# A one-core block of WKV, 1-bit FFN, cross attention and ternary layer: the last attention's first 256 tokens ahead, two norms rearranged, half of the boot's weight sums on VectorE

## The chip, the cores and the metric

The kernel runs on one core of one Trainium2 chip. Its engines are TensorE (PE in the profile, with its weight loads as PEld), VectorE (DVE), ScalarE (ACT), GpSimd (POOL) and SyncE (SP), which issues the DMAs. The metric is the device time of one execution in microseconds (us), lower is better. Before the change the median of three runs is 1129.53 us (1128.88 to 1131.5).

## The reference

Four residual layers over `x` of (4, 512, 512), that is batch, tokens, channels, with a context of the same shape. Cut to what is computed:

```python
x = x + tanh(g_xattn[0]) * wkv(w, u, layernorm(x), ctx)        # scan over the tokens, each channel by itself
x = x + tanh(g_ffn[0])   * ffn_1bit(layernorm(x), w1, w2, w3)
x = x + tanh(g_xattn[1]) * attention_int8(layernorm(x), ctx)
x = x + tanh(g_ffn[1])   * ternary(x, gamma, W)

# ffn_1bit: bitlinear(x, w) = quant(x) @ (sign(w) * mean|w|).T
#           quant: groups of 64 channels, int8 by the group's max
#           h = silu(bitlinear(x, w1)) * bitlinear(x, w2); bitlinear(h, w3)
# attention_int8: q = qdq(x) @ qdq(wq).T + bq; k, v = split(ctx @ wkv.T + bkv)
#           16 heads of 32; softmax(q k^T / sqrt(32)) v; qdq(o) @ qdq(wp).T + bp
# ternary:  rms = rsqrt(mean(x*x) + 1e-6); xn = x * rms * gamma
#           a_scale = 127 / (max|xn| + 1e-5); round(xn * a_scale) / a_scale
#           @ (W rounded to -1, 0, 1 by mean|W|).T
```

The hidden width of the FFN is 2048; w1, w2 and w3 are fp32, 4 MB each.

## The kernel before

**Tiles and stages.** A batch's 512 tokens are four tiles `t` of 128 tokens by 512 channels, held in `xb`. The four batches go through WKV, FFN, attention and the ternary layer; neighbouring layers of neighbouring batches overlap. The first part, the boot, also makes the weights: `Weights.fetch` loads pieces `(m, f)` of 1 MB of w1, w2, w3 (m = 0, 1, 2; f = 0 to 3) into the tile `wn` (two buffers), `signs` writes the signs, `magnitudes` sums |w| with four ACT Abs passes with accumulation (L331), `turned` transposes the signs (`wt_ps`, L316 on ACT or L318 on DVE) and stores them to `wD`. `up_scales` needs the sums of all pieces of w1 and w2: `mean` adds them on DVE (L370), TensorE adds over the partitions (`tot_ps`), and L365 and L376 make the scales that the FFN's first activation needs. `Context.load(b)` transposes the context (`ct_ps`, L455); `keys_values(b)` makes keys (`k_ps`, split by ACT L272 and DVE L273, stored to `kD`) and values (`v_ps`, L534, stored to `vD`), and the attention loads them from there.

**WKV.** `wkv_layer` takes chunks of 128 channels: exponentials on ACT, scans on DVE (L625), the quotient (L631, L636), then TensorE transposes the chunk's result back (`wy_ps`) and DVE adds it to `xb` (L644). After chunk 3 come the layer norm's statistics and `rsqrt`, and with its scale and shift `ln_r` (L219, L220) ACT makes `ff_xn` (L224). The FFN quantises it (L231 group maxima, L671 to int8, ACT L675 back to bf16, POOL L676 times the scale), transposes it (`tp_ps`) and multiplies (`ff_hp`).

**Norm helpers.** `layernorm` makes statistics (L207, L210), a variance (L213, L214) and `rsqrt`: a shift and a subtraction as the first guess, then three Newton steps, all small DVE operations (L185 to L195). `centred` applies scale and shift on ACT (L224), `centred_aside` on POOL (L228). `absmax` is a DVE reduction (L231). `rounded` (ACT L246) multiplies by a scale and adds a magic number, `transposed_rows` transposes on TensorE (`qr_ps`) and takes the number off again (ACT L253).

**Attention.** `prepared` normalises a tile on POOL, takes absmax, rounds and transposes it; `project(g)` makes two head pairs of queries and stores them to `qD`. A unit `(p, h)` is a pair of heads p (0 to 7) over one half h of the tokens: 16 units per batch, in the order (0,0), (0,1), (1,0) and so on. The loop runs k = 0 to 17 and does in turn `scores(k)` (`s_ps`, DVE max L938, ACT exp L940), `values(k-2)` (`o_ps`, ACT copy L980), `turned(k-1)` (`pt_ps`, copied by ACT L960 and, in the last batch, by DVE L958 for one head of each pair) and `collect(k-2)` (`ot_ps`, DVE reciprocal L996 and product L998 into `at_o`). Each k has four yields. Keys of a pair are loaded by `fetch_keys` (tile `at_kR`, two buffers) when the pair before them has its h = 0; queries two units ahead; values for two pairs at a time. `project_out(t)` quantises `at_o` and multiplies by the output weights (`p_ps`), makes `at_y` (L1031) and adds it to `xb` (L1032), on POOL for batches 0 to 2, on DVE for the last.

**Ternary layer.** `ternary(t)` makes `tf_xn`: centred with scale and shift (POOL L228, in the last batch ACT L224), times gamma (L1110, POOL or, in the last batch, DVE), then absmax into `tf_s` (L231), small steps (L1115 to L1118), `rounded`, `transposed_rows`, `f_ps`, and L1128 with the store. For batches 0 to 2 this runs beside the next batch's layers; for the last batch `end((0, 1))` and `end((2, 3))` do `project_out`, layer norm and ternary for two tiles each, staggered by one step, after the unit loop. So after the last collect both halves of the tokens are still to be done.

**What sets the order.** A hand-made planner runs generators. Each has due places: `at_us` and `at_unit` for the boot, and slots (1/17 of a batch) afterwards; `run` always takes the generator whose next step is due first. TensorE's instructions are chained in that order in groups (`next_turn`). The other engines' order is made by a scheduler, but instructions given to `tc.keep_in_program_order` stay where the program has them. Each engine executes its own list in order, so an instruction that waits holds those behind it.

Of the kernel before, what the change touches and what calls it, by code (L numbers as in the profile page):

```python
# [10 lines left out]
F32 = mybir.dt.float32  # L11
# [19 lines left out]
def kernel(  # L31
# [150 lines left out]
    def rsqrt(v, n):  # L182
# [13 lines left out]
            y = y2  # L196
        return y

    def layernorm(xb, rms=False, tiles=range(NT), pinned=False):
# [20 lines left out]
        nc.vector.scalar_tensor_tensor(r[:, 1, :], mv[:, :, 0], -1.0, y, ALU.mult, ALU.mult)  # L220
        return {t: (r[:, 0, i : i + 1], r[:, 1, i : i + 1]) for i, t in enumerate(tiles)}
# [5 lines left out]

        nc.gpsimd.tensor_scalar(dst, xb[:, t, :], r[t][0], r[t][1], ALU.mult, ALU.add)  # L228

    def absmax(dst, src):  # L230
        nc.vector.tensor_reduce(dst, src, AX.X, ALU.max, apply_absolute_value=True)  # L231

    def quantise(dst, src, rscale, lo, hi=127.0):

# [56 lines left out]
    class Weights:  # L291
# [35 lines left out]
        def magnitudes(self, m, f, after=None):  # L327

            wn = self.raw.pop((m, f))
            for j in range(NC):  # L330
                ins = nc.scalar.activation(  # L331
                    wn[:, j, :],
                    wn[:, j, :],
                    AF.Abs,
                    accum_out=self.asum[:, m, f, j : j + 1],
                )
                if after is not None:
                    behind(ins, after)
# [492 lines left out]
    def attention_layer(b, xb, pool, tiles=range(NT)):  # L831
# [18 lines left out]
        def prepared(t, r):  # L850
            xn = row("at_xn")
            centred_aside(xn, xb, r, t)
            s = sm.tile([P, 2], F32, name="at_s", tag="at_s")
            yield True
            absmax(s[:, 0:1], xn)
            int8_scale(s[:, 0:1], s[:, 1:2], s[:, 0:1])
            rounded(xn, s[:, 1:2])
            yield True
            transposed_rows(xqT[:, :, t * P : (t + 1) * P], xn)
            sp = bank("sx_ps")[:, 0:P]  # L860
            transpose(sp, s[:, 0:1].to_broadcast([P, P]), ident)
# [47 lines left out]
            return slice(64 * (p % 2), 64 * (p % 2) + 64)  # L909

        def fetch_keys(p):
            kR[p] = pool.tile([P, 2, T], F32R, name="at_kR", tag="at_kR")
            stack(kR[p], kD[b][p // 2][:, pair(p), :], (0, 1, 0, 1))

# [8 lines left out]
            nc.sync.dma_start(out=V[g], in_=vD[b][:, :, g * P : (g + 1) * P])  # L923

        units = [(p, h) for p in range(NP) for h in range(len(tiles) // 2)]

        def scores(k, i, t):

# [86 lines left out]
        def project_out(t):  # L1015
            s = sm.tile([P, 2], F32, name="at_s", tag="at_s")
            o = o_all[:, t, :]
            absmax(s[:, 0:1], o)
            int8_scale(s[:, 0:1], s[:, 1:2], s[:, 0:1])
            rounded(o, s[:, 1:2])  # L1020
            yield True
            oqT = pool.tile([P, NC, P], BF16, name="at_oqT", tag="at_oqT")
            transposed_rows(oqT, o)
            yield True
            pp = bank("p_ps")
            for c in range(NC):
# [3 lines left out]
            y = row("at_y")  # L1030
            nc.vector.scalar_tensor_tensor(y, pp, s[:, 0:1], swp_b, ALU.mult, ALU.mult)  # L1031
            (nc.vector if alone else nc.gpsimd).tensor_tensor(  # L1032
                xb[:, t, :], xb[:, t, :], y, ALU.add
            )
            yield True
# [9 lines left out]
        def end(ts):  # L1045

            yield from together([project_out(t) for t in ts])
            r = layernorm(xb, rms=True, tiles=ts)
            yield from together([ternary(b, xb, pool, t, r) for t in ts])


        ahead, behind_it = end((0, 1)), end((2, 3))
        ending = in_steps([ahead, behind_it], 1)

        for k in range(len(units) + 2):
            now, before = k < len(units), 0 < k <= len(units)
# [10 lines left out]
            if alone and k > len(units):  # L1069
                next_turn()  # L1070
                next(ahead)
            yield
            for i in range(2):
                if now:
                    scores(k, i, 1)
            yield
            for i in range(2):
                if before:
                    turned(k - 1, i, 1)
            next_turn()  # L1080
            if k > 1:
                collect(k - 2)
            if now:
                p, h = units[k]
                if h == 0:
                    if p + 1 < NP:
                        fetch_keys(p + 1)
                    if p % 2 == 0 and p // 2 + 2 < NC:
                        next_turn()
                        project(p // 2 + 2)  # L1090
                elif p % 2 and p // 2 + 1 < NC:
                    fetch_values(p // 2 + 1)
                if k + 2 < len(units):
                    fetch_queries(k + 2)
            yield
# [7 lines left out]
    def ternary(b, xb, pool, t, r):  # L1103

        last = b == NB - 1
        if r is None:
            r = layernorm(xb, rms=True, tiles=[t])
        xn = pool.tile([P, D], F32, name="tf_xn", tag="at_row", bufs=ROWS)
        (centred if last else centred_aside)(xn, xb, r, t)
        (nc.vector if last else nc.gpsimd).tensor_tensor(xn, xn, gamma_b, ALU.mult)  # L1110
        s = sm.tile([P, 3], F32, name="tf_s", tag="tf_s")
        if not last:
            yield True
        absmax(s[:, 0:1], xn)
        nc.vector.tensor_scalar(s[:, 0:1], s[:, 0:1], 1e-5, None, ALU.add)  # L1115
        nc.vector.reciprocal(s[:, 1:2], s[:, 0:1])
        nc.vector.tensor_scalar(s[:, 1:2], s[:, 1:2], 127.0, None, ALU.mult)
# [3 lines left out]
        xT = pool.tile([P, NC, P], BF16, name="tf_xT", tag="at_oqT")  # L1121
        transposed_rows(xT, xn)
        yield True
        fp = bank("f_ps")
# [5 lines left out]
        yield True  # L1130

    def ternary_layer(b, xb, pool):
        r = layernorm(xb, rms=True)
        yield from in_steps([ternary(b, xb, pool, t, r) for t in range(NT)], 1)

# [42 lines left out]
    with (  # L1178
# [19 lines left out]
        def at_unit(n):  # L1198
# [98 lines left out]
    for b in range(NB):  # L1297
        if b:
# [12 lines left out]
            (b + 1 + 1.7 / SLOTS, b + 1 + 3.7 / SLOTS, 4),  # L1311
            (b + 1 + 3.75 / SLOTS, b + 1 + 4.35 / SLOTS, 2),
            (start, end, 72),
            (end, end + 2.4 / SLOTS, 6),
            (end + 2.4 / SLOTS, end + 3.4 / SLOTS, 4),
        )
        if b < NB - 1:
            line(
                late(lambda b=b: ternary_layer(b, xs[b], at)),
                (end + (3 if b < NB - 2 else 4.5) / SLOTS, end + (8 if b < NB - 2 else 12) / SLOTS, 7),  # L1320
                aside=True,
            )
    run(NB + 9)

# [44 lines left out]
```

## Time and profile before

| what | value |
|---|---|
| median of three runs | 1129.53 us (1128.88 to 1131.5) |
| the profiled execution, its own time | 1129.12 us |
| its span in the trace | 1127.3 us |
| mean granted TensorE clock | 0.954 |
| PE / PEld busy | 962.9 / 678.1 us |
| DVE / ACT / POOL busy | 877.7 / 721.4 / 308.8 us |
| first FFN matmul of batch 0 (`ff_hp` on the chain) | 102.31 us |
| last collect of batch 3 (`at_o` L998) starts | 1091.27 us |

The span is cut into 40 slices of 28.2 us in the page's second part, and each digit there is a busy share in tenths. "Idle before" an instruction is the time its engine stood, with what ended it. In the chain of waits each line is a start, a length, and the engine and line that held the end up. Busy shares over the whole span average over stages with different limits, so the stages are read by windows.

The last attention's 16 units end, by the start of the collecting DVE product, at 1004.00, 1010.08, 1015.24, 1020.74, 1026.16, 1032.44, 1042.96, 1049.16, 1055.68, 1061.88, 1068.02, 1073.34, 1079.10, 1084.54, 1088.85 and 1091.27 us.

### The profile page before, as it was taken

How to read it: one execution, taken by the hardware profiler on the slowest of the kernel's cores; microseconds unless marked ns; L12 is line 12 of the kernel's file. 1: busy time of each engine (PE TensorE's matmuls, PEld its weight loads, DVE VectorE, ACT ScalarE, POOL GpSimd, SP SyncE). 2: the span in 40 equal slices, each digit the busy share in tenths (PEclk: the TensorE clock that was granted, in tenths of full speed). 3: DMA queues.
4: the chain of work that ended last, by engine and by line, in shares of the span. 5: the costliest groups of instructions: out<-in, count | busy, mean ns of one | idle time of the engine just before them, and what ended most of it. 6: DMA issues, size and time to landing. Idle time of an engine off the chain costs nothing.

```text
span 1127.3 us, 16575 instructions
## 1 busy us (share of the span) xinstructions
PE 962.9 (85%) x5548; PEld 678.1 (60%) x5548; DVE 877.7 (78%) x1885; ACT 721.4 (64%) x1482; POOL 308.8 (27%) x301
## 2 busy tenths in 40 slices
PE   3878898988878978899998797999999899888983
PEld 2344565555546656676776475777777677555651
DVE  5857547769877799998769899978689766688776
ACT  5677655453224677667767676777676677877763
POOL 3821004333104143531215536212122400112000
PEclk9888999998888999999999999999999999998996
DMA  8188854443434654645555554464674572333401
GB/s 279 38 291 302 295 193 150 177 177 149 149 120 151 225 189 155 217 159 175 191 187 182 164 182 169 152 208 150 218 214 146 187 233 60 113 104 104 130 2 38
DMA packets 85668, 189.58 MB, mean 168 GB/s; under 512 B 12240, under 2 KB 36816, under 8 KB 74576
## 3 DMA queue, kind: packets, MB, share of 16 engines
q1 hardware_dynamic: 85584, 188.53, 49.7%
q8 instruction: 44, 0.72, 0.3%
q14 instruction: 40, 0.33, 0.1%
HBM read 148.65 MB, written 39.85 MB: 167 GB/s over the span
## 4 chain that ended last, share of the span: by engine, by line
PE 43%; DVE 29%; ACT 13%; issue 5%; POOL 4%; DMA 4%; SPq 1%; ACTq 0%; POOLq 0%; DVEq 0%
PE ff_hp L168 13%; PE ff_acc L168 6%; PE pt_ps L171 5%; PE o_ps L168 4%; DVE at_nm L938 3%; PE v_ps L168 3%; DVE wk_q L631 3%; PE s_ps L168 3%; ACT at_P L940 3%; DVE qg_i L671 2%; PE tp_ps L171 2%; ACT at_PT L960 2%; PE qr_ps L171 2%; ACT wk_e L603 1%; DMA wn<-in_L_ffn_w_dram 1%
## 5 line engine op out<-in xcount | busy, mean ns | idle before, releaser
L168 PE MATMUL ff_hp<-wT,xp 128*128 128x512 f32 x1024 | 272.3, 410 | 3.1 <-ACT at_P L940 2.1
L168 PEld LDWEIGHTS ff_hp<-wT,xp 128*128 128x128 f32 x1024 | 195.4, 195 | 51.9 <-ACT at_P L940 4.4
L940 ACT ACTIVATE at_P<-s_ps,at_nm 128x512 f32<-128x512 f32 x256 | 174.8, 690 | 64.8 <-DVE at_nm L938 63.4
L938 DVE TENSOR_REDUCE at_nm<-s_ps 128x1 f32<-128x512 f32 x256 | 165.8, 677 | 27.1 <-PE s_ps L168 26.7
L676 POOL TENSOR_TENSOR ff_z<-qg_b,qg_s 128x512 f32<-128x512 bf16 x64 | 71.2, 1112 | 378.9 <-ACT qg_b L675 326.3
L171 PE MATMUL pt_ps<-ident,at_P 128*128 128x128 f32 x1024 | 142.0, 279 | 12.5 <-ACT at_os L980 5.1
L960 ACT COPY at_PT<-pt_ps 128x512 f32<-128x512 f32 x224 | 125.0, 596 | 39.1 <-PE pt_ps L171 38.4
L171 PEld LDWEIGHTS pt_ps<-ident,at_P 128*128 128x128 f32 x1024 | 113.9, 141 | 54.7 <-issue 13.9
L168 PE MATMUL ff_acc<-wT,hr 128*128 128x512 f32 x512 | 136.7, 408 | 6.3 <-DVE hr L688 3.3
L168 PE MATMUL s_ps<-at_kR,at_qR 128*128 128x512 f32 x256 | 97.2, 448 | 19.9 <-ACT at_P L940 12.7
L168 PEld LDWEIGHTS ff_acc<-wT,hr 128*128 128x128 f32 x512 | 92.4, 190 | 27.4 <-DVE hr L688 4.6
L736 ACT ACTIVATE ff_z<-ff_hp,coef 128x512 f32<-128x512 f32 x64 | 43.9, 686 | 68.7 <-PE ff_hp L168 65.6
L168 PE MATMUL o_ps<-at_PT,at_V 128*32 128x256 f32 x1024 | 72.6, 397 | 1.6 <-ACT at_PT L960 0.9
L675 ACT CAST qg_b<-qg_i 128x512 bf16<-128x512 int8 x80 | 49.4, 617 | 34.2 <-DVE qg_i L671 24.7
L741 DVE SCALAR_TENSOR_TENSOR ff_z<-ff_hp,coef,ff_z 128x512 f32<-128x512 f32 x64 | 47.6, 744 | 28.3 <-PE ff_hp L168 28.1
L168 PE MATMUL v_ps<-wkvT,cT 128*128 128x512 f32 x128 | 63.4, 643 | 5.0 <-DVE wT L318 1.8
L168 PEld LDWEIGHTS s_ps<-at_kR,at_qR 128*128 128x128 f32 x256 | 45.6, 194 | 35.9 <-ACT at_P L940 20.7
L168 PE MATMUL k_ps<-cT,wkvT 128*128 128x512 f32 x128 | 62.3, 637 | 3.1 <-ACT cT L455 1.4
L737 DVE SCALAR_TENSOR_TENSOR ff_z<-ff_z,ff_hp 128x512 f32<-128x512 f32 x64 | 43.5, 679 | 25.7 <-ACT ff_z L736 25.7
L687 ACT CAST hr<-tp_ps 128x512 fp32r<-128x512 f32 x64 | 37.6, 588 | 33.9 <-PE tp_ps L171 33.9
L631 DVE RECIPROCAL wk_q<-wk_q 128x256 f32<-128x256 f32 x32 | 54.3, 1718 | 1.4 <-POOL wk_p L619 1.4
L171 PE MATMUL tp_ps<-ident,ff_z 128*128 128x128 f32 x256 | 40.3, 281 | 14.9 <-ACT at_PT L960 5.8
(177 smaller groups left out, 1749.7 us busy)
## 6 DMA issues: line engine op xcount, KB each, us to landing
wT<-wD SPq DMA_DIRECT2D x72, 1024.0 KB, 5.3
wn<-in_L_ffn_w_dram SPq DMA_DIRECT2D x18, 1024.0 KB, 7.3
at_kR<-kD SPq DMA_DIRECT2D x128, 128.0 KB, 3.5
at_qR<-qD SPq DMA_DIRECT2D x256, 64.0 KB, 2.2
wD<-wT SPq DMA_DIRECT2D x12, 1024.0 KB, 4.5
kD<-k_half SPq DMA_DIRECT2D x16, 512.0 KB, 3.3
qD<-at_half SPq DMA_DIRECT2D x32, 256.0 KB, 2.1
cn<-in_ctx_dram SPq DMA_DIRECT2D x8, 512.0 KB, 5.9
```

The lines of the kernel that those rows point to most:

```text
L168: return in_turn(nc.tensor.matmul(*args, **kwargs))
L171: return in_turn(nc.tensor.transpose(*args))
L631: nc.vector.reciprocal(half, half)
L675: nc.scalar.copy(qb, qi)
L676: nc.gpsimd.tensor_tensor(grouped(src), grouped(qb), s.unsqueeze(2).to_broadcast([P, NG, GS]), ALU.mult)
L687: nc.scalar.copy(part[:, 0, :], pt)
L736: nc.scalar.activation(z, hp, AF.Tanh, scale=coef[:, 0:1])
L737: nc.vector.scalar_tensor_tensor(z, z, 1.0, hp, ALU.add, ALU.mult)
L741: nc.vector.scalar_tensor_tensor(z, hp, coef[:, 1:2], z, ALU.mult, ALU.mult)
L938: nc.vector.tensor_reduce(nm, sp, AX.X, ALU.max, negate=True)
L940: nc.scalar.activation(lanes[k, i, t], sp, AF.Exp, bias=nm, accum_out=sums[k][:, t, i : i + 1],)
L960: made[k] = nc.scalar.copy(dst, blocks(pt))
```

## The change

It has four parts.

1. In the boot, the pieces (0,2), (1,1) and (1,3) are summed by one DVE reduction over 128 x 2048 in place of four ACT passes, and the due places of the second context's transposes (50 to 62.2), its keys (57 to 75 becomes 66.5 to 78.5) and the first two sign transposes (49 to 56.5, 58 to 63) are later. TensorE's order so has the last WKV chunk's transposes (`wy_ps`) right after the first piece's `wt_ps`, ahead of `ct_ps` and `k_ps`.
2. `absmax` in `prepared` and in the ternary layers of batches 0 and 1 is kept in program order, and so are the statistics of those ternary layers.
3. In the last attention the last eight units are (4,0), (5,0), (6,0), (7,0), (7,1), (4,1), (5,1), (6,1), so that the first 256 tokens are complete four units before the end. `next_keys` fetches the next pair that isn't resident, which brings three more fetches of 4 DMAs of 128 KB. `aside` does steps of `end((0, 1))` inside the loop: one at the end of k = 13, one at the end of k = 14, and two in the middle of k = 15; after the loop come one step of it, one of `end((2, 3))`, one more of it, and the rest of `end((2, 3))`.
4. The ternary layer of batches 2 and 3 is written anew: `statistics` gives minus the mean and the reciprocal root apart; `tf_xn` is (x - mean) * gamma in one DVE instruction, its absmax doesn't need the root, and the root goes into the scales instead. In batch 2, `at_y` is added on DVE, `project_out` is spread over 4.8 slots instead of 2.4, and the ternary layer is due at other places. For tiles 2 and 3 of the last batch the root's Newton steps run on POOL (`rsqrt_aside`, 12 instructions of 128 x 2), beside DVE's `tf_xn` and absmax.

The diff, cut:

```diff
+    def rsqrt_aside(v, n):
...
+        for _ in range(3):
+            t = sm.tile([P, n], F32, name="rs_t", tag="rs_t")
+            nc.gpsimd.tensor_tensor(t, v, y, ALU.mult)
+            nc.gpsimd.tensor_tensor(t, t, y, ALU.mult)
+            nc.gpsimd.tensor_scalar(t, t, -0.5, 1.5, ALU.mult, ALU.add)
+            y2 = sm.tile([P, n], F32, name="rs_y", tag="rs_y")
+            nc.gpsimd.tensor_tensor(y2, y, t, ALU.mult)
+            y = y2
+        return y
...
-    def absmax(dst, src):
-        nc.vector.tensor_reduce(dst, src, AX.X, ALU.max, apply_absolute_value=True)
+    def absmax(dst, src, pinned=False):
+
+        ins = nc.vector.tensor_reduce(dst, src, AX.X, ALU.max, apply_absolute_value=True)
+        if pinned:
+            tc.keep_in_program_order(ins)
...
             wn = self.raw.pop((m, f))
+
+            if f and m < 2 and (m + f) % 2 == 0:
+                nc.vector.tensor_reduce(
+                    self.asum[:, m, f, :], wn, AX.X, ALU.add, apply_absolute_value=True
+                )
+                return
...
         units = [(p, h) for p in range(NP) for h in range(len(tiles) // 2)]
+        if alone:
+
+            units[-8:] = [(p, h) for h in range(2) for p in ((4, 5, 6, 7), (7, 4, 5, 6))[h]]
+        resident = []
+
+        def next_keys(k):
+
+            for j in range(k + 1, len(units)):
+                p = units[j][0]
+                if p not in resident:
+                    if resident[0] not in [u[0] for u in units[k + 1 : j]]:
+                        fetch_keys(p)
+                    return
...
-            r = layernorm(xb, rms=True, tiles=ts)
-            yield from together([ternary(b, xb, pool, t, r) for t in ts])
+            means, scale = statistics(b, xb, ts)
+            yield from together([ternary(b, xb, pool, t, means, scale) for t in ts])
...
-        ending = in_steps([ahead, behind_it], 1)
+
+        def aside(k, i):
+            for _ in range({(-3, 1): 1, (-2, 1): 1, (-1, 0): 2}.get((k - len(units), i), 0)):
+                if alone:
+                    next_turn()
+                    next(ahead)
...
         if alone:
-            yield from ending
+            for one in (ahead, behind_it, ahead):
+                next_turn()
+                next(one)
+                yield
+            yield from behind_it
...
+    def statistics(b, xb, tiles):
...
+        y = rsqrt_aside(v, n) if b == NB - 1 and tiles[0] else rsqrt(v, n)
+        m = sm.tile([P, n], F32, name="ln_m", tag="ln_m")
+        nc.vector.tensor_scalar(m, mv[:, :, 0], -1.0, None, ALU.mult)
...
+        if last:
+            nc.vector.scalar_tensor_tensor(
+                xn, xb[:, t, :], r[t], gamma_b, ALU.add, ALU.mult
+            )
+            absmax(s[:, 0:1], xn)
+            nc.vector.tensor_scalar(s[:, 0:1], s[:, 0:1], scale[t], 1e-5, ALU.mult, ALU.add)
+        else:
+            centred_aside(xn, xb, r, t)
+            nc.gpsimd.tensor_tensor(xn, xn, gamma_b, ALU.mult)
             yield True
-        absmax(s[:, 0:1], xn)
-        nc.vector.tensor_scalar(s[:, 0:1], s[:, 0:1], 1e-5, None, ALU.add)
+            absmax(s[:, 0:1], xn, pinned=True)
+            nc.vector.tensor_scalar(s[:, 0:1], s[:, 0:1], 1e-5, None, ALU.add)
...
-        event(at_us(50.0), lambda: context.load(1))
+        event(at_us(62.2), lambda: context.load(1))
...
-            (at_us(57.0), at_us(75.0), 4),
+            (at_us(66.5), at_us(78.5), 4),
...
-        for m, us in ((0, 49.0), (1, 58.0)):
+        for m, us in ((0, 56.5), (1, 63.0)):
...
-            (end, end + 2.4 / SLOTS, 6),
+            (end, end + 2.4 / SLOTS, 6)
+            if b != NB - 2
+            else (end - 0.15 / SLOTS, end + 4.65 / SLOTS, 6),
```

More of the change, by code (lines that the diff above doesn't have):

```diff
@@ L197, in rsqrt @@
         return y
+    def rsqrt_aside(v, n):
+        half = sm.tile([P, n], I32, name="rs_half", tag="rs_half")
+        nc.vector.tensor_scalar(half, v.bitcast(I32), 1, None, ALU.logical_shift_right)
+        y = sm.tile([P, n], F32, name="rs_y", tag="rs_y")
+        nc.vector.tensor_scalar(
+            y.bitcast(I32), half, -1.0, float(0x5F3759DF), ALU.mult, ALU.add
+        )
[8 more added lines that the diff above has]
+        return y
     def layernorm(xb, rms=False, tiles=range(NT), pinned=False):
@@ L911, in fetch_keys @@
         def fetch_keys(p):
+            resident[:] = resident[-1:] + [p]
             kR[p] = pool.tile([P, 2, T], F32R, name="at_kR", tag="at_kR")
@@ L1029, in project_out @@
                 )
-            y = row("at_y")
+            if b > NB - 3:
+                y = wk.tile([P, D], F32, name="at_y", tag="wk_v")
+            else:
+                y = row("at_y")
             nc.vector.scalar_tensor_tensor(y, pp, s[:, 0:1], swp_b, ALU.mult, ALU.mult)
-            (nc.vector if alone else nc.gpsimd).tensor_tensor(
+            (nc.vector if b > NB - 3 else nc.gpsimd).tensor_tensor(
                 xb[:, t, :], xb[:, t, :], y, ALU.add
@@ L1068, in attention_layer @@
                     turned(k - 1, i, 0)
-            if alone and k > len(units):
-                next_turn()
-                next(ahead)
+            aside(k, 0)
             yield
@@ L1084, in attention_layer @@
                 p, h = units[k]
[L1085 to L1091, printed above, removed]
+                next_keys(k)
+                if h == 0 and p % 2 == 0 and p // 2 + 2 < NC:
+                    next_turn()
+                    project(p // 2 + 2)
+                if p % 2 and h == (0 if alone else 1) and p // 2 + 1 < NC:
                     fetch_values(p // 2 + 1)
@@ L1094, in attention_layer @@
                     fetch_queries(k + 2)
+            aside(k, 1)
             yield
         if alone:
-            yield from ending
+            for one in (ahead, behind_it, ahead):
+                next_turn()
+                next(one)
+                yield
+            yield from behind_it
         else:
             yield from in_steps([project_out(t) for t in tiles], 1)
[L1103 to L1110, printed above, removed]
-        s = sm.tile([P, 3], F32, name="tf_s", tag="tf_s")
-        if not last:
+    def statistics(b, xb, tiles):
+        n = len(tiles)
+        mv = sm.tile([P, n, 2], F32, name="mv", tag="mv")
+        for i, t in enumerate(tiles):
+            s6 = sm.tile([P, 6], F32, name="s6", tag="s6")
+            tc.keep_in_program_order(nc.vector.bn_stats(s6, xb[:, t, :]))
+            nc.vector.bn_aggr(mv[:, i, :], s6)
+        v = sm.tile([P, n], F32, name="ln_v", tag="ln_v")
+        nc.vector.tensor_scalar(v, mv[:, :, 1], LN_EPS, RMS_EPS, ALU.add, ALU.mult)
+        nc.vector.tensor_tensor(v, v, mv[:, :, 1], ALU.add)
+        y = rsqrt_aside(v, n) if b == NB - 1 and tiles[0] else rsqrt(v, n)
+        m = sm.tile([P, n], F32, name="ln_m", tag="ln_m")
+        nc.vector.tensor_scalar(m, mv[:, :, 0], -1.0, None, ALU.mult)
+        at = {t: slice(i, i + 1) for i, t in enumerate(tiles)}
+        return {t: m[:, at[t]] for t in tiles}, {t: y[:, at[t]] for t in tiles}
@@ new lines, in ternary @@
+    def ternary(b, xb, pool, t, r, scale=None):
+        last = b > NB - 3
+        if last:
+            xn = ff.tile([P, D], F32, name="tf_xn", tag="ff_a", bufs=3)
+        else:
+            xn = pool.tile([P, D], F32, name="tf_xn", tag="at_row", bufs=ROWS)
+        s = sm.tile([P, 3], F32, name="tf_s", tag="tf_s")
+        if last:
+            nc.vector.scalar_tensor_tensor(
+                xn, xb[:, t, :], r[t], gamma_b, ALU.add, ALU.mult
+            )
+            absmax(s[:, 0:1], xn)
+            nc.vector.tensor_scalar(s[:, 0:1], s[:, 0:1], scale[t], 1e-5, ALU.mult, ALU.add)
+        else:
+            centred_aside(xn, xb, r, t)
+            nc.gpsimd.tensor_tensor(xn, xn, gamma_b, ALU.mult)
@@ L1113, in ternary @@
             yield True
-        absmax(s[:, 0:1], xn)
-        nc.vector.tensor_scalar(s[:, 0:1], s[:, 0:1], 1e-5, None, ALU.add)
+            absmax(s[:, 0:1], xn, pinned=True)
+            nc.vector.tensor_scalar(s[:, 0:1], s[:, 0:1], 1e-5, None, ALU.add)
         nc.vector.reciprocal(s[:, 1:2], s[:, 0:1])
-        nc.vector.tensor_scalar(s[:, 1:2], s[:, 1:2], 127.0, None, ALU.mult)
+        if last:
+            nc.vector.tensor_scalar(
+                s[:, 1:2], s[:, 1:2], scale[t], 127.0, ALU.mult, ALU.mult
+            )
+        else:
+            nc.vector.tensor_scalar(s[:, 1:2], s[:, 1:2], 127.0, None, ALU.mult)
@@ L1120, in ternary @@
         yield True
-        xT = pool.tile([P, NC, P], BF16, name="tf_xT", tag="at_oqT")
+        if last:
+            xT = ring.tile([P, NC, P], BF16, name="tf_xT", tag="w")
+        else:
+            xT = pool.tile([P, NC, P], BF16, name="tf_xT", tag="at_oqT")
         transposed_rows(xT, xn)
@@ L1132, in ternary_layer @@
     def ternary_layer(b, xb, pool):
-        r = layernorm(xb, rms=True)
-        yield from in_steps([ternary(b, xb, pool, t, r) for t in range(NT)], 1)
+        if b == NB - 2:
+            r, scale = statistics(b, xb, range(NT))
+            yield
+        else:
+            r, scale = layernorm(xb, rms=True, pinned=True), None
+        yield from in_steps([ternary(b, xb, pool, t, r, scale) for t in range(NT)], 1)
     def next_batch(b):
@@ L1319 @@
                 late(lambda b=b: ternary_layer(b, xs[b], at)),
-                (end + (3 if b < NB - 2 else 4.5) / SLOTS, end + (8 if b < NB - 2 else 12) / SLOTS, 7),
-                aside=True,
+                (end + 3 / SLOTS, end + 8 / SLOTS, 7)
+                if b < NB - 2
+                else (end + 4.85 / SLOTS, end + 11.85 / SLOTS, 7),
+                aside=b < NB - 2,
             )
```

## The prediction

> **What bounds the kernel now.** I read the page first, then the waits by engine, the chain of waits in two stretches, and windows by stage. The page's slices:
>
> ```profile
> PE   3878898988878978899998797999999899888983
> DVE  5857547769877799998769899978689766688776
> PEclk9888999998888999999999999999999999998996
> ```
>
> TensorE is the bound on the whole (962.9 us of 1127.3), but not where the change works: in the first slices, in the 35th to 37th (8 tenths, the first half of the last attention) and in the last (3) it has holes. Windows (start:end, length, then busy time of PE, PE's weight loads, DVE, ACT, POOL, then the granted clock, DMA share and GB/s):
>
> ```profile
> 70.00:80.00 10.00, 5.41 (x29) 4.11 (x30) 1.35 (x2) 7.73 (x20) 0.00 (x0) 0.66 0.86 279
> ...
> 90.00:100.00 10.00, 6.04 (x16) 2.75 (x15) 5.26 (x18) 8.83 (x22) 1.55 (x1) 0.91 1.04 408
> ...
> 1020.00:1040.00 20.00, 15.64 (x114) 10.12 (x114) 15.41 (x55) 14.66 (x37) 8.06 (x8) 0.84 0.41 117
> 1040.00:1091.00 51.00, 46.25 (x381) 30.75 (x379) 37.73 (x74) 35.54 (x91) 0.00 (x0) 1.00 0.24 73
> ...
> 1100.00:1110.00 10.00, 2.22 (x9) 1.72 (x10) 9.31 (x35) 3.72 (x5) 0.00 (x0) 0.58 0.00 0
> ```
>
> At 70 to 100 us ACT and the DMA engines are full and PE is not. At 1040 to 1091, the last attention's second half, PE is the bound (46.25 of 51) and DVE has 13.3 us free. From 1091 on DVE is the bound and PE stands. The chain in the first part (start, length, what):
>
> ```profile
> 63.16 7.71 DMA wn<-in_L_ffn_w_dram
> ...
> 81.83 8.15 DMA wn<-in_L_ffn_w_dram
> ...
> 97.74 1.56 POOL ff_xn L676
> ...
> 100.46 0.23 PE tot_ps L168 x2
> ```
>
> So the first FFN matmul (102.31) hangs on weight pieces, on the Abs passes behind them and on ff_xn. DVE's waits for POOL (us in all, times, longest):
>
> ```profile
> DVE tf_s L231 <- POOL tf_xn L1110: 6.0, 6, 2.3
> ...
> DVE at_s L231 <- POOL at_xn L228: 4.4, 4, 1.7
> ```
>
> And the chain of the tail:
>
> ```profile
> 1091.27 0.29 DVE at_o L998
> ...
> 1102.10 0.07 DVE ln_r L220
> ...
> 1117.59 0.82 ACT tf_xn L246
> ...
> 1120.42 2.75 PE f_ps L168 x8
> ```
>
> From the last collect's end (1091.56) to the end (1127.3) is 35.7 us, in which two chains, tiles 0,1 and then tiles 2,3, run one after the other on DVE.
>
> **The change, part by part.** All against the profiled run: 1129.12, span 1127.3, so 1.8 outside; the median is 0.4 above it.
>
> *First part.* Three pieces lose four Abs with their accumulator reads on ACT (4 x (0.62+0.19) = 3.2 alone, 2.3 to 2.6 in a row as the chain shows); each gets one DVE reduce of 128x2048. The row w_am has 2.28 for that shape: 6.8 us on DVE, which from 70 to 80 was busy 1.35 of 10. Chunk 3's wy_ps transposes go ahead of context 1's ct_ps and k_ps: their row of input, DVE's L636, ended at 67.8, but they ran at 82.7, so 14.9 us are there to win locally. What eats them: the DVE is in order. Its xb adds (L644), context V's adds and the statistics stand behind the reduce of (0,2), which landed at 70.9 (+2.28 = 73.2); statistics to 78; the rsqrt chain is behind the reduce of (1,1), one landing later, about 79.2+2.3 = 81.5; ln_r at 84 for 90.7. On ACT ff_xn is behind the Abs of (1,2). On SP the piece (1,1) is now issued ahead of batch 1's x (1 MB), and wD and kD stores move behind; at 8 us per MB, and a DMA share near 1, I put (1,2)'s landing at 86.5 for 90.0, ff_xn at 90.2 for 93.2. Last, (1,3)'s reduce sits in order behind a qi that waits for qg_b and POOL's product: it ends at 97 to 99.3; tot_ps 99.5 for 100.46, first ff_hp 99 to 100.5. Bounds: 0 (the landings don't move; DMA share is 1.04 already), -5 (ff_xn follows ln_r by what it does now). I take -2, near the first, as the DMA rows are full. What is late next: k_ps and kD of context 1, needed by batch 1's attention, which comes after batch 0's (from 347 us on): nothing.
>
> *Pinned absmax, batches 0 to 2.* Each at_xn and tf_xn reduce (0.68) now stands where it is written, a step after POOL's 0.77 and 1.29, so that DVE doesn't stand in front of POOL. Of the 10.4 us waited, 1.8 are batch 2's tf_xn (next part); 8.6 are left. Cover: they cost PE only where it runs out, as in the 3.2 us before pt_ps at 888. Bounds -7 (nearly all) and +1 (a pinned reduce, 0.68, now stands ahead of an at_nm once or twice). A third: -3. Behind a waiting absmax were at_nm, then exp on ACT, then pt_ps.
>
> *Last attention's body, units 0 to 12, with batch 2's ternary beside it.* POOL loses 4 centrings (0.77), 4 products (1.29) and 4 adds (1.3), 13.4 us; DVE gains 4 adds x 0.68 and 4 fused centre-and-gamma x 0.74 = 5.7 and loses the 1.8 waited. Units 5 to 6 took 10.5 us from collect to collect where 6.2 is usual beside this work (collects of at_o 1032.44, 1042.96), with PE waiting 3.6 on tf_xn: 4.3 to win. Batch 2's project_out is spread over 4.8 slots for 2.4, 2.9 us more room for PE. Against it DVE's load at 998 to 1020 is 19.49 of 22. Bounds -7 (4.3+2.9, all) and +2 (5.7 with no cover, less 3.7 of the stall). I take -3. The new unit order adds three fetches of key pairs, 12 DMAs of 128 KB on SP. Each is issued over one unit (5.3 us) before its s_ps, and such a load lands in 3.5, at a DMA share of 0.24: hidden. Without that cover one s_ps would wait up to 3.5. Queries are fetched two units ahead as now; values, now at h = 0, one unit or more ahead.
>
> *Units 13 to 17.* Here tiles 0 and 1 get project_out, statistics and ternary's start. DVE by rows: 2 absmax 1.3, 2 y 1.5, 2 adds 1.4, 2 bn_stats 1.4, rsqrt and small 2.6 (as 1099.36 to 1102.0), part of it in gaps, 2 xn 1.5, 2 absmax 1.3: 9.5 to 11 in about 3 units, where DVE had 13.3/51 x 16 = 4.2 idle plus some. PE gets 16 transposes (1.2) and 8 p_ps (2.1), ACT 2 roundings (1.6) ahead of an exp. In DVE's written order y waits for p_ps, at_nm behind it, exp behind that. I get +4.5 (DVE surplus 9.5-5) to +8.5 (adding 1.8 for the late exp and 2.2 for the last two collects); +6.6 taken.
>
> *Tail.* After the last collect only tiles 2,3 have a chain: absmax to p_ps as now, y at +7.0 (now +10.5, behind the rsqrt of tiles 0,1, and f_ps of 0,1 comes first on PE), y, add, y, add, bn_stats to +11.4. Then DVE runs xn and absmax (to +14.6) while POOL runs 12 dependent operations of 128x2. No row has these; bounds per operation 0.10 (POOL's memset of 128x1) and 0.77 (its 128x512 tensor_scalar). At 2 elements I go near the first, 0.12 and a gap of 0.08 as DVE has: 2.4, so +15.8. Rounding at +16.6 for +26.0 now; the rest, 9.7, stays. 26.3 for 35.7: -9.4. At 0.77 the chain takes 9.2 and 6.8 of this goes. The trace has POOL at 1.29 for a 128x512 product where DVE takes 0.69.
>
> [...]
>
> At the end PE's clock counts too: 0.58 in 1100 to 1110, and f_ps x8 took 2.75 where p_ps x8 at full clock took 1.90. A shorter hole can win 0.8; left out.
>
> The Trainium skill (TensorE: Matmul & The Clock Gate, What's actually happening) has the clock halve after an idle window of about 3.4 us; PE's hole in the changed tail is longer than that, so by the page the 0.8 is not won, and by the row it is open.
>
> Sum: -2 -3 -3 +6.6 -9.4 = -10.8; 1129.1-10.8 = 1118.3, against the median 1118.7.
>
> **Rivals.**
> 1. *It is hidden or given back.* DMA holds the first part (0), PE has other cover in the middle (-1), DVE is full in the body (-1), units 13 to 17 cost 8.5 against 9.4: -2.9, 1126.6 (1124 to 1130). For: DMA share 1.04, DVE 19.49 of 22. Against: the 4.3 us stall is plainly POOL's.
> 2. *All pays.* -5 -7 -7 and 4.5-9.4: -23.9 is the extreme; with two of three at it, about -18 to -23: 1106 to 1112. For: PE is the bound, so each hole closed counts. Against: PE windows of 46.25 in 51 leave little.
> 3. *Slower: DVE held in order in units 13 to 17.* Each of the four written steps makes DVE wait for the chain ahead of it: 3.8 (1091.27 to 1095.05), 7.0 (to 1102.1), 5.9 (to 1108.0), 3.7 (to 1111.76): 20.4 in all if nothing of attention runs beside it. Less 9.4 it is +11, so 1129.1+11-8 = 1132 with the other parts as forecast. It decides from 17.4 us of stall on (9.4+8). For: the collects of this part already hang on DVE. Against: the steps are set a half unit or more apart, longer than each link.
>
> **How the numbers follow.** Forecast 0.52, with its own range 1112 to 1126 (the bounds above, not all at one end); rival 1 0.20, rival 2 0.15, rival 3 0.13. 0.2%, 2.3 us, is about what can be told from no change. Faster: 0.52+0.15+half of 0.20 = 0.77; same: 0.2 x 0.4 + 0.02 = 0.10; slower 0.13. Leaving out half of rival 2 and most of rival 3: 1108 to 1130.5.
>
> **What would show it.** First ff_hp at 99 to 100.5 and DVE waiting for wn; no DVE wait on tf_xn for batch 2, and fewer for 0 and 1; collects of units 5 and 6 about 6 apart; units 13 to 15 some 6.6 longer together; 26 us from the last at_o to the end, with POOL's 12 operations in about 2.4. Wrong if POOL's take over 0.9 each, if the landing of (1,2) is later than 90, or if the last four collects lie more than 9 us later than the body's gain allows.

## The result and the profile after

The changed kernel takes 1149.53 us (median of five, 1148.83 to 1152.12) where the kernel before takes 1129.65 in the same comparison: the ratio is 1.0165, 95% interval 1.0139 to 1.0191, that is some 19 us slower. Its profiled execution took 1148.83 us with a span of 1147.0. The prediction, 1118.7 in a range of 1108 to 1130.5, is wrong, and on the wrong side.

TensorE's slices in the changed kernel look like those of before; the average hides the loss:

```profile
PE   3879898887877878889997876999999899887884
```

Where the time went is read by laying TensorE's instructions of the two traces side by side, each against the same one of before. The table gives how much later (+) they run at a few places (time of the kernel before), medians over 20 us:

| place, us | 100 | 300 | 360 | 640 | 700 | 840 | 920 | unit 11's collect (1073) | last collect (1091) | end |
|---|---|---|---|---|---|---|---|---|---|---|
| changed kernel | -4.5 | -3.7 | +2.2 | +2.7 | +15.5 | +15.1 | +19.4 | +21.4 | +29.3 | +19.7 |

So the boot gained what was hoped and more, and the tail what was hoped (29.3 to 19.7). Three steps lost it: 6 us at 340 to 360 (inputs of batch 0's attention), 13 at 665 to 700 (batch 0's ternary layer), 4 at 880 to 910 (batch 1's). In these stretches the change pins instructions and does nothing else. The waits of TensorE in the changed kernel (what for, us in all, times, longest):

```profile
PE qr_ps L171 <- ACT tf_xn L267: 22.6, 6, 10.8
...
PE qr_ps L171 <- ACT at_xn L267: 7.8, 3, 4.1
```

And before:

```profile
PE qr_ps L171 <- ACT tf_xn L246: 17.6, 4, 8.0
...
PE qr_ps L171 <- ACT at_xn L246: 3.4, 2, 2.2
```

Of the waits on `tf_xn`, 11.2 us of the 22.6 and 14.0 of the 17.6 lie in the tail, behind the last collect. In the layers ahead of it they grew from 3.6 to 11.4. DVE's waits for POOL, which the pins were counted on to shorten, did get shorter, 10.4 to 5.4. Of these 5.0 us, 1.8 are batch 2's, whose norm left POOL; the pins' share is `at_s`, 4.4 to 0.9, while `tf_s` of batches 0 and 1 waits 4.5 where it waited 4.2. The wait went over to TensorE.

How, shows DVE's timeline at the inputs of batch 0's attention, first of before, then of the changed kernel (start, length, line, operation, shapes):

```profile
346.13 1.29 DVE L688 TENSOR_TENSOR xp<-tp_ps,xp 128x512 fp32r<-128x512 f32 x2
347.33 1.27 DVE L231 TENSOR_REDUCE at_s<-at_xn 128x1 f32<-128x512 f32 x2
```

```profile
342.41 1.29 DVE L715 TENSOR_TENSOR xp<-tp_ps,xp 128x512 fp32r<-128x512 f32 x2
343.62 1.28 DVE L187 TENSOR_SCALAR rs_y<-rs_half 128x2 int32<-128x2 int32 x1
...
347.80 0.15 DVE L238 SCALAR_TENSOR_TENSOR ln_r<-mv,rs_y 128x2 f32<-128x2 f32 x1
347.87 0.68 DVE L764 SCALAR_TENSOR_TENSOR ff_z<-ff_z,ff_hp 128x512 f32<-128x512 f32 x1
348.47 0.68 DVE L250 TENSOR_REDUCE at_s<-at_xn 128x1 f32<-128x512 f32 x1
```

Before, the absmax follows `xp` at once, 1.2 us behind its start. Pinned, it starts 6.1 us behind it, 4.9 later, after the whole root of the next two tiles and an FFN step: its place in the program is one planner step behind the POOL instruction, and that step holds all this. Two of the root's steps take 1.28 and 1.20 us there, where the others take 0.16; they stand beside two adds of POOL (see the last section), and 2.2 of the 4.9 us are theirs. The rounding, and `qr_ps` on TensorE, whose place is fixed, wait for the absmax.

The same at batch 0's ternary layer. The root on DVE, its first and last instruction before:

```profile
655.61 0.16 DVE L213 TENSOR_SCALAR ln_v<-mv 128x4 f32<-128x4 f32 x1
...
663.51 0.15 DVE L220 SCALAR_TENSOR_TENSOR ln_r<-mv,rs_y 128x4 f32<-128x4 f32 x1
```

And in the changed kernel:

```profile
664.33 0.16 DVE L231 TENSOR_SCALAR ln_v<-mv 128x4 f32<-128x4 f32 x1
...
666.71 1.22 DVE L647 TENSOR_TENSOR_SCAN wk_q<-wk_e 128x512 f32<-128x512 f32 x1
...
670.48 2.32 DVE L652 TENSOR_TENSOR_SCAN wk_p<-wk_e 128x512 f32<-128x512 f32 x1
...
674.40 1.22 DVE L192 SCALAR_TENSOR_TENSOR rs_t<-rs_y,ln_v 128x4 f32<-128x4 f32 x1
675.54 0.68 DVE L715 TENSOR_TENSOR hr<-tp_ps,hr 128x512 fp32r<-128x512 f32 x1
...
679.10 0.15 DVE L238 SCALAR_TENSOR_TENSOR ln_r<-mv,rs_y 128x4 f32<-128x4 f32 x1
```

The pinned statistics begin the root later, when WKV's scans of the next batch stand in DVE's list; the root takes 14.8 us instead of 7.9. Some 4.3 of these 14.8 are six steps that run beside POOL's WKV and FFN work and take 0.48 to 1.22 us where they take about 0.15 otherwise. `hr` stands between the root's steps, and TensorE's waits from 660 to 720 us are these:

```profile
PE qr_ps L171 <- ACT tf_xn L267: 6.3, 2, 5.9
PE pt_ps L171 <- DVE hr L715: 3.7, 1, 3.7
PE pt_ps L171 <- DVE xb L671: 3.5, 1, 3.5
```

Together they are 13.5 us, where before `f_ps` waited 2.5 for `hr` and `qr_ps` 1.3 for `tf_xT`: the greater part of the step of 13 in the table. `xb` (L671) is the add of WKV's result. The runs below tell the pins apart: with the statistics alone pinned (e2) the waits on `hr` and `xb` are there, 3.7 and 3.4, and with the absmaxes alone (e3) that on `tf_xn` is, 4.7. With no pins (e1) `pt_ps` waits 0.3 for `hr` and not for `xb`, and `f_ps` waits its 2.5 again.

The boot went by the prediction's steps, only sooner. Its chain in the changed kernel, then DVE's three reductions:

```profile
86.49 10.36 PE k_ps L168 x24
...
97.28 0.13 PE tot_ps L168 x2
...
99.08 1.88 PE ff_hp L168 x7
```

```profile
69.25 2.29 DVE L353 TENSOR_REDUCE asum<-wn 128x4 f32<-128x2048 f32 x1 [0.47 <-DMA wn<-in_L_ffn_w_dram]
...
79.42 2.29 DVE L353 TENSOR_REDUCE asum<-wn 128x4 f32<-128x2048 f32 x1 [1.92 <-DMA wn<-in_L_ffn_w_dram]
...
94.23 2.28 DVE L353 TENSOR_REDUCE asum<-wn 128x4 f32<-128x2048 f32 x1
```

From 86.5 us on the chain is nearly all TensorE's own work, the keys `k_ps` that the new due places put there, where before it ran from the landing of a weight piece at 89.99 over ACT and POOL to `ff_hp`. And the tail, from the chain of waits (last collect's end is 1120.86):

```profile
1120.89 1.28 DVE at_s L250 x2
...
1127.24 0.76 DVE at_y L1075
...
1132.08 0.17 DVE ln_v L1162
...
1134.00 0.20 POOL rs_t L209
...
1137.97 0.82 ACT tf_xn L267
...
1140.80 2.46 PE f_ps L168 x8
```

26.2 us from the last collect to the end, where 35.7 were before and 26.3 were forecast; the steps at +6.4 (y), +11.2 (variance), +17.1 (rounding) answer to +7.0, +11.4 and +16.6.

### The profile page after: what moved, and what is told of

Its sections match the earlier page's. It is cut to its first block, busy times and chain, and to the rows that moved or that the text cites. A ratio compares the mean times of both kernels' runs of the same rounds, so it can differ in the third digit from the quotient of the medians.

```text
span 1147.0 us, 16542 instructions
## 1 busy us (share of the span) xinstructions
PE 967.9 (84%) x5548; PEld 682.7 (60%) x5548; DVE 892.3 (78%) x1884; ACT 712.9 (62%) x1454; POOL 299.1 (26%) x301
## 4 chain that ended last, share of the span: by engine, by line
PE 49%; DVE 26%; ACT 14%; issue 5%; DMA 4%; POOL 2%; SPq 0%; POOLq 0%; DVEq 0%; ACTq 0%
PE ff_hp L168 14%; PE ff_acc L168 7%; PE pt_ps L171 6%; PE s_ps L168 4%; PE o_ps L168 3%; PE v_ps L168 3%; ACT at_P L981 3%; PE k_ps L168 3%; DVE at_nm L979 2%; DVE wk_q L658 2%; PE qr_ps L171 2%; DVE qg_i L698 2%; PE tp_ps L171 2%; DMA wn<-in_L_ffn_w_dram 2%; ACT at_PT L1001 1%
## 5 line engine op out<-in xcount | busy, mean ns | idle before, releaser
L171 PEld LDWEIGHTS pt_ps<-ident,at_P 128*128 128x128 f32 x1024 | 114.5, 142 | 64.2 <-issue 14.8
L168 PE MATMUL ff_acc<-wT,hr 128*128 128x512 f32 x512 | 139.7, 415 | 6.3 <-DVE hr L715 3.3
L168 PEld LDWEIGHTS s_ps<-at_kR,at_qR 128*128 128x128 f32 x256 | 46.7, 197 | 40.3 <-ACT at_P L981 26.2
L168 PE MATMUL v_ps<-wkvT,cT 128*128 128x512 f32 x128 | 65.9, 664 | 5.1 <-DVE wT L339 1.8
```

The source lines that it names most:

```text
L168: return in_turn(nc.tensor.matmul(*args, **kwargs))
L171: return in_turn(nc.tensor.transpose(*args))
```

## The experiments

Each was timed against the kernel before on its own chip; ratios are to that. All but e4, e9, e10, e14 and e17 start from the changed kernel.

**e1, e4: the pins away, the pins alone.** e1's edit, and e4 does the reverse to the kernel before:

```diff
-            absmax(s[:, 0:1], xn, pinned=True)      # prepared, ternary
+            absmax(s[:, 0:1], xn)
-            r, scale = layernorm(xb, rms=True, pinned=True), None
+            r, scale = layernorm(xb, rms=True), None
```

`statistics`, new in the change, also keeps its statistics (batches 2 and 3) in program order; it does so still in e1 and in what is built on e1.

> The changed kernel with no absmax kept in program order, nor the statistics of the ternary layers of batches 0 and 1; all else as changed. Against the kernel before, TensorE's instructions run 6 us later by 360 us, 13 more by 700, 4 more by 905. Theory P (these pins cost it): about 23 us of the 1149.5 go, 1123 to 1130. Rival R (the boot's new places and the last attention shift the layers against each other, the pins are innocent): 1145 to 1150.

> The kernel before with the pins alone: the absmaxes of at_xn and of the ternary layers of batches 0 and 1, and these layers' statistics, kept in program order. Theory P: 1129.5 plus about 23, 1149 to 1155. Rival R: 1128 to 1132. The forecast on record put these edits at -3 with bounds of -7 and +1.

e1: 1127.19 us, ratio 0.9964 (0.9943 to 0.9985). e4: 1154.09, ratio 1.0204 (1.0171 to 1.0237), 23 us for a few instructions held in their place. The product of the two, 1.0167, is the changed kernel's 1.0165. Theory P holds, R falls. In e4's trace TensorE loses 6 us by 360, 10 between 640 and 700, 4 by 905: the same three steps. DVE's waits for the pinned absmaxes there are 0.9 (`at_s`, before 4.4) and 6.3 (`tf_s`, before 6.0); TensorE's, on the roundings behind them, grew:

```profile
PE qr_ps L171 <- ACT tf_xn L249: 27.4, 7, 8.0
...
PE qr_ps L171 <- ACT at_xn L249: 8.0, 3, 4.2
```

That is 14.4 us more than before, for 3.2 us less on DVE. The waits on `hr` and `xb` at batch 0's ternary layer are there too, 3.7 and 3.5.

**e2, e3, e15: which pins.** From e1, one kind of pin is put back at a time:

```diff
+            r, scale = layernorm(xb, rms=True, pinned=True), None      # e2
+            absmax(s[:, 0:1], xn, pinned=True)      # e3: prepared and ternary; e15: prepared alone
```

> As e1, but with the ternary layers' statistics of batches 0 and 1 kept in program order. In the changed kernel their root starts at 664.3 and ends at 679.1, 14.8 us through WKV's scans, where before it ended at 663.5. Theory S (the late statistics are what costs 13+4 at 700 and 905): e1 plus 13 to 18. Rival X (the pinned absmaxes cost it): e1 plus 0 to 2.

> As e1, but with the absmaxes of the attention's inputs and of the ternary layers of batches 0 and 1 kept in program order, and the statistics free. Theory S: e1 plus about 6 (the loss at 340 to 360, where the absmax of at_xn now stands behind the next pair's root), so 1132 or so. Rival X: e1 plus 20 to 23. If both together are needed, e2 and e3 both give little.

> As e1, with the absmax of at_xn alone kept in program order. In e3 TensorE lost 6.1 us between 330 and 360 us, at batch 0's inputs, and some 1 to 2 at each of 430, 600, 690 and 900. Theory Q (the inputs' absmax, one step late behind the next pair's root, is the larger part of e3's 9.9): e1 plus 6 to 8. Rival Z (the ternary layers' absmax is): e1 plus 0 to 3.

e2: 1136.16, ratio 1.0056 (1.0034 to 1.0078), 9.0 us over e1 by the medians and 10.4 by the ratios. e3: 1137.1, 1.0040 (1.0008 to 1.0072), 9.9 and 8.6 us. e15: 1132.51, 1.0021 (0.9999 to 1.0043), which is 0.0057 or 6.4 us over e1. So both kinds of pin cost: the statistics 9 to 10, the attention's inputs 6, and the ternary layers' absmaxes, not run alone, what is left of e3, 2 to 4, which the intervals don't tell from nothing. Together this is some 19 of the 22 to 23 us that all of them cost; the intervals, 2 to 4 us to either side, leave room for the rest. S was right about the place of the root and too high for its size (9 to 10 instead of 13 to 18); X alone falls; Q holds. In e2 the root runs from 657.26 to 672.04, again 14.8 us; in e1 it ended at 660.9.

**e6, e9: the boot.** e6 takes from e1 the reduction and the four due places; e9 gives them alone to the kernel before.

```diff
-            if f and m < 2 and (m + f) % 2 == 0:      # e6, from e1
-                nc.vector.tensor_reduce(...)
-                return
-        event(at_us(62.2), lambda: context.load(1))
+        event(at_us(50.0), lambda: context.load(1))
...
```

> As e1, and the boot as before: four Abs passes for every piece, old due places. In e1 TensorE ran 4.6 us earlier than before at 300 us, 2.6 at 600 and 1.4 at 980. If what is lost on the way is absorbed by waits that come anyway (theory G, given back): e1 plus 1 to 2. If the boot's gain reaches the end whole (rival K): e1 plus 4 to 5.

> The kernel before with the boot's part alone (three DVE reductions, new due places). The forecast on record gave -2, bounds 0 and -5. In the changed kernel the first ff_hp came 3.4 us earlier and TensorE was 4.4 ahead at 100 us; e6 lost 5.2 us against e1 when this part was taken away. Theory K: 3 to 5 less than before. Rival G (the lead is used up by waits later): 0 to 2 less.

e6: 1132.26, 1.0010 (0.9995 to 1.0026), 5.2 us over e1. e9: 1128.29, 0.9959 (0.9937 to 0.9981), 4.6 us less than before. K holds: the boot's lead reaches the end.

**e5, e10, e12: batch 2's end on DVE.** e5 gives e1 the old form and due places back, e10 gives the kernel before the new ones alone, e12 moves only the adds back to POOL.

```diff
-        last = b > NB - 3                              # e5; reversed in e10
+        last = b > NB - 2
-            (nc.vector if b > NB - 3 else nc.gpsimd).tensor_tensor(     # e5 and e12
+            (nc.vector if b > NB - 2 else nc.gpsimd).tensor_tensor(
...
```

> As e1 (no pins, 1127.2), and batch 2's attention end and ternary layer as before the change: y added and norm made on POOL, project_out over 2.4 slots, ternary due at 4.5 to 12. In e1 the collects of units 1 to 11 of the last attention took 68.3 us where before they took 63.2, and ACT waited 3.9 us for at_nm behind a Newton step. Theory D (DVE, given the adds, the fused norms and an absmax, holds at_nm back): 3 to 6 less than e1, 1121 to 1124. Rival W (the new unit order or its key fetches slow the body): within 1.5 of e1.

> The kernel before with batch 2's new attention end and ternary layer alone (adds and fused norm on DVE, new due places). The forecast on record took -3 for the body, bounds -7 and +2. By e7, where units 0 to 11 lost 3.3 us of the lead they began with although the stall between units 5 and 6 was POOL's before: +2 to +4. If the forecast's mechanism holds (the 4.3 us stall goes): -2 to -4.

> As e1, with batch 2's four adds of y on POOL again (4 x 0.69 us off DVE, 4 x 1.3 onto POOL). In e1 DVE was busy 10.00 of 10 us at 1020 to 1030 and TensorE 7.30. Theory D (DVE's load is what the body loses): e1 minus 1 to 3. Rival O (the order of DVE's list in a few places counts, not its load): within 1 of e1, or worse.

e5: 1133.26, 1.0030 (1.0007 to 1.0052), 7 us slower than e1, not 3 to 6 faster: D and W fall. In its trace DVE stands for 3 us in an absmax that waits for POOL, with at_nm behind it, and TensorE waits 8.05 once for `at_P`; units 4 to 5 take 15.1. e10: 1130.28, 0.9982 (0.9961 to 1.0002): about -2.0, near the forecast's -3, and no change is not excluded. e12: 1128.63, 0.9974 (0.9954 to 0.9994), 1 us over e1: the load of four adds decides nothing.

**e7, e8, e11: the last units and the tail.**

```diff
-            units[-8:] = [(p, h) for h in range(2) ...]                # e7: natural order, old staggering
-        y = rsqrt_aside(v, n) if b == NB - 1 and tiles[0] else rsqrt(v, n)   # e8
+        y = rsqrt(v, n)
-            for _ in range({(-3, 1): 1, (-2, 1): 1, (-1, 0): 2} ...    # e11
+            for _ in range({(-3, 1): 1, (-2, 1): 1, (-1, 1): 2} ...
```

> As e1, with the last attention's units in the old order and both halves of the tokens finished after the last collect; the new statistics and fused norm stay. By e1 against before, units 12 to 15 take 6.1 us more and the stretch after the last collect 9.6 less: if that is the whole of it, e1 plus 3.5. Rival N (the new norm alone shortens the end, the order brings nothing): e1 within 1.

> As e1, with the last two tiles' Newton steps on DVE. On POOL the 12 took 3.24 us in e1 (0.19 each and 0.08 between), and DVE waited 2.17 of it. On DVE nine take 1.8, but in order with two absmaxes of 0.65: 0 to 0.5 less than e1 if DVE's gaps hold nothing, 0.5 to 1 more if they collide. Both within 1 us of e1: then POOL or DVE is the same for this step.

> As e1, with the two steps of tiles 0 and 1 that stand in the middle of k = 15 put at its end. In e1 the collect of unit 13 comes 9.7 us after that of unit 12, where before it came 5.4 after; y, adds and statistics lie between two at_nm of DVE there. Theory H (they hold the scores' maxima back): the 9.7 falls by 2 or more, and the stretch after the last collect grows by less: e1 minus 0 to 2. Rival T (the tail then waits for tiles 0 and 1): e1 plus 1 to 4.

e7: 1130.04, 0.9991 (0.9975 to 1.0007), 3 us over e1 as forecast, though e18 below doesn't repeat it. e8: 1127.81, 0.9963 (0.9942 to 0.9984), e1's time: POOL or DVE is the same for the root. e11: 1132.42, 1.0008 (0.9990 to 1.0025), 5 us over e1: unit 13 falls from 9.7 to 5.9 as H says, but units 14 and 15 take 2.6 more and the stretch after the last collect grows from 26.5 to 32.5: T, a little beyond its range.

**e13, e14, e16, e17, e18: do the parts add up?** The boot alone gives -4.6, batch 2's end alone -2.0, but e1, with the last attention's part too, -4. e14 joins the first two; e13 spreads the fused norms on DVE between the scores' maxima; e16 and e18 put the second key pair's fetch, which `next_keys` leaves one unit late, back to k = 0 (in e1 and in e7); e17 adds the unit order to e14, with that fetch.

```diff
+            if b == NB - 2:                        # e13: behind the newest at_nm
+                behind(ins, tops[-1])
-                    if resident[0] not in [u[0] for u in units[k + 1 : j]]:      # e16, e17, e18
+                    if len(resident) < 2 or resident[0] not in [u[0] for u in units[k + 1 : j]]:
```

> As e1, with each of batch 2's four fused norms ordered on DVE behind the newest at_nm of the last attention, so that one norm and one absmax stand between two pairs of maxima; in e1 two norms and two absmaxes stand ahead of a pair, and units 4 and 5 take 9.0 and 9.6 us. Theory O (the order of DVE's list loses what the parts gain alone): units 4 and 5 fall to 5.7 to 8, and the time to e1 minus 2 to 5. Rival L (DVE's load, whatever its order): within 1 of e1.

> The kernel before with two parts, the boot's and batch 2's new ternary layer; e9 gave 0.9959 of before and e10 0.9982. If they add up: 0.994, some 1124 to 1126. If the lead of the boot is used up in batch 2's stretch: 0.996 to 0.998.

> As e1, with the second key pair of each attention fetched at k = 0 as before the change; next_keys leaves it to k = 1, because the only pair resident then is still needed. With it, DVE's list in the last attention has four at_nm between the first and the second of batch 2's fused norms, as e14 has, where e1 has none. Theory V (the late first key load turns DVE's list, and the list loses 3 to 4 us): units 4 falls from 9.0 to about 6 and the time to e1 minus 3 to 5, some 0.992 of before. Rival L (list and load don't matter here): within 1 of e1.

> e14 (boot and batch 2, 0.992 of before) with the new order of the last eight units and the steps of tiles 0 and 1 ahead, the first key load as in e16, and the last batch's norm as before (ACT centring, root on DVE before the norm). By e1 against e14, units 12 to 15 cost 6.1 and the end gains 7.0; with the old norm the end is longer by the root, 2 to 3: e14 plus 0 to 3. If the order pays for itself: e14 minus 1 to 3.

> As e7 (natural order of the units, the new norm in the last batch, no pins) with the first key load as in e16. If V holds, e7's 0.9991 falls by some 0.004 to 0.995, and against e16 it shows what the order of the units is worth when DVE's list is the same: e16 plus 2 to 4.

e14: 1122.86, 0.9920 (0.9895 to 0.9944), the fastest of all, 9 us less than before: the two parts add up. The sum of the two alone is 6.6, and the intervals don't tell 9 from it. e13: 1129.87, 0.9981 (0.9962 to 1.0001): units 4 and 5 take 9.6 and 7.5 and the next two 7.4 and 7.8; the time moves along and none is won, so O in this form falls. e16: 1130.21, 0.9982 (0.9961 to 1.0002): unit 4 did fall from 9.0 to 5.7, as V says, but the time didn't fall with it. V falls as an explanation of the time. e17: 1134.48, 1.0028 (1.0011 to 1.0044), 12 us over e14: the unit order doesn't pay for itself with the old norm. e18: 1127.04, 0.9964 (0.9944 to 0.9984), 2 us less than e16, the reverse of e7 against e1.

So the unit order, in three pairs, was worth -3 (e1 against e7), +2 (e16 against e18) and, with the old norm, some +12 (e17 against e14). Each interval is some 0.002 wide to either side, so the first two can't be told from zero; the third is clear. In the traces its terms are plain: from unit 11's collect to the last, e1 takes 24.2 us where e14 takes 17.9, and from the start of the last collect to the end 26.45 for 33.45. It buys 7.0 for 6.2. This gain needs both the order and the new norm: the end takes 35.1 with the new norm alone (e7) and 32.7 with the order alone (e17). So e17 pays for the order (23.8 for 17.9) and gets 0.7 for it; that is 5 of its 12 us, and the rest lies ahead of unit 11.

Why e1, with all of e14's parts and this one, is 0.0044 slower than e14 stays open. Part of it lies in units 1 to 11 (68.2 us in e1, 65.0 in e14); DVE is full there in both, and the two lists differ though the text is the same. The windows of the two, e14 and then e1 (columns as in the prediction):

```profile
1020.00:1030.00 10.00, 8.26 (x66) 5.93 (x62) 10.00 (x31) 7.51 (x19) 0.00 (x0) 1.00 0.44 112
```

```profile
1020.00:1030.00 10.00, 7.30 (x65) 4.61 (x53) 10.00 (x32) 4.40 (x12) 0.00 (x0) 1.00 0.39 111
```

DVE is busy 10.00 of 10 in both; in e14 ACT gets to work 7.51 and in e1 4.40. The maxima that feed it come later in e1's list; that this costs the time is not shown, since e16, where unit 4 falls to 5.7 as in e14, was no faster than e1.

## Why the prediction was wrong, by its own steps

**Pinned absmax: this step failed.** It was put at -3 with bounds of -7 and +1, and measured +23 (e4). Three things were wrong in it. It counted the wait that would go (8.6 of 10.4 us on DVE) and what stands behind the waiting absmax there, and never followed who needs the pinned instruction's result: the rounding, and `qr_ps`, fixed in TensorE's order. The upper bound was priced as one reduction of 0.68 in front of an at_nm, where the price is the distance to the program's place, 4.9 us at 343 to 348. And the statistics that the same edit pins, named under the change, got no term at all: 9 to 10 us by e2. The prediction argued that the pinned reduction "stands where it is written, a step after POOL's"; it didn't ask what that step contains. The gain was not there either: `tf_s` waits as long as before. (The 3.2 us that it reads as standing before `pt_ps` at 888 stand, in the trace, before `tp_ps` at 891.64.)

**Boot: mechanism right, size low.** -2 was taken, bounds 0 and -5; e9 gives -4.6 and e6 5.2. The reductions ended at 71.54, 81.71 and 96.51 for 73.2, 81.5 and 97 to 99.3; ln_r at 84.0 for 84. The mis-sized term is the landing of the piece (1,2), 86.5, and ff_xn behind it, 90.2. SP issues that piece at 77.03 and batch 1's 1 MB of x at 77.46, behind it, where the prediction had only (1,1) ahead of x; ACT's timeline has the piece's Abs at 83.13, at once behind its own casts, so it had landed by then, and ff_xn at 87.13:

```profile
81.53 1.64 ACT L337 CAST wT<-wt_ps 128x512 fp32r<-128x512 bf16 x3
83.13 0.63 ACT L358 ACTIVATE wn<-wn 128x512 f32<-128x512 f32 x1
...
87.13 1.52 ACT L242 ACTIVATE ff_xn<-xb,ln_r 128x512 f32<-128x512 f32 x2
```

The ff_hp that stands at 102.31 in the chain of before started at 99.08, for 99 to 100.5.

**Body: size off, sign as forecast but not settled.** -3 was taken; e10 gives -2.0 (-4.4 to +0.2). In the changed kernel it isn't there: TensorE was 19.3 late at 960 us and 21.4 at unit 11's collect. From unit 4's collect to unit 5's and on to unit 6's it takes 8.8 and 8.5 us, where 6.3 and 10.5 were before: the stall is spread, not shorter, and units 2 and 3 take 2.8 more.

**Units 13 to 17: right.** +6.6 was taken; from unit 11's collect to the last the changed kernel takes 25.8 for 17.9, +7.9, e1 +6.2. The price is DVE's in-order list, as the step says: with two of the steps moved behind (e11), unit 13 falls from 9.7 to 5.9.

**Tail: right.** -9.4 was taken, -9.5 measured. Inside it POOL's 12 operations took 3.24 us for 2.4, each 0.19 and 0.08 between (bounds 0.10 and 0.77); DVE waited 2.17 for them, and e8 shows no gain in having them on DVE instead. TensorE had no matmul from 1130 to 1138 us, its granted clock from 1138 to 1141 was 0.50, and `f_ps` x8 took 2.46 us for 2.75: of the 0.8 us that was left open, 0.3 came.

**The sum.** Without the pins' term the forecast is -7.8; e1 measured -4.1 (-6.4 to -1.7), so the other terms together were too hopeful as well; the body's gain is not in e1's trace, where units 1 to 11 take 68.2 us for 63.3 before. The rivals: 1 was right on how little the end brings net, wrong on the boot; 2 is excluded; 3 named an in-order DVE as the slow case, which is the kind of cause that decided, but put it in units 13 to 17, where it cost 7.9 and not 20.4. Of the signs named beforehand, the first ff_hp, the waits for `wn` and the tail came, and of the waits on `tf_s` those of batch 2 went; fewer of them in batches 0 and 1 (3 before, 3 now) and collects of units 5 and 6 about 6 apart did not come.

## What to carry to other kernels

A wait is worth what stands behind it on its own engine, and an instruction is worth who waits for its result: an edit that fixes an order has to be priced at both. Pinning an instruction where the program has it costs the whole distance to where a scheduler would have put it, and everything that the program has in between; list the instructions between the two places and add them up before calling a pin cheap. And take a bundle of edits apart: here two of four parts together (e14) beat both kernels, with 0.9920 of before.

## What the runs showed of the hardware that was not expected

Some DVE operations grow while POOL works. The 128x2 steps of the root take 0.16 us, but 1.28 and 1.20 at 343.62 and 344.93, while POOL ran two 128x512 adds, 343.59 to 344.87 and 344.83 to 346.11: each step ended within 0.03 us of an add's end. The next step, at 346.16, took 0.16 again. The subtraction at 348.58 of the kernel before took 1.26 beside one of the same adds. Size doesn't decide: in the changed kernel's trace `wk_e<-wk_e,wk_q` (128x512) takes 0.68 us alone and 1.38 beside a POOL instruction of over 0.4 us (medians of 10 and 6), `qg_i<-ff_z,qg_r` 0.69 and 1.17 (50 and 14). These, and most of the root's steps, read two tensors from SBUF. Operations that read one, or one of their two from TensorE's results, kept their time: `at_nm` 0.68 and 0.68 (189 and 67), `hr<-tp_ps,hr` 0.68 and 0.68 (41 and 23), the pinned absmaxes 0.68. That isn't the whole rule, since the subtraction reads one tensor and grew; no run varied it.

The Trainium skill (GPSIMD Engine Reference, 3.1 Elementwise) gives about 156 ns of dispatch for an instruction of VectorE and no number for GpSimd's. This case's 128x2 steps take 0.16 us on DVE, about that figure, and 0.19 on POOL, with 0.277 from one start to the next. That section's rule to keep elementwise work on VectorE made no difference for these 12 steps, since e8 took e1's time.

The executions of one kernel lie up to 12 us apart here (the kernel before beside e1: 1126.2 to 1138.65 in 25; e9: 1121.31 to 1131.21), and the traces show it in steps: the boot's lead over the one trace of before was between 1.3 and 5.3 us at 120 us in kernels with the same boot, and steps of 1.3 to 1.7 us come or don't come near 500, 600 and 700 us. A single profile can't be read to better than that.
